# Cross-attention on one core: a third plain fp32 value unit in the first batch, its head's loads exchanged between two queues, first and last batch in a new order

## The chip, the core and the metric

One core of a Trainium2 chip runs the whole kernel: TensorE (PE: matrix products; PEld is its weight load), VectorE (DVE), ScalarE (ACT), GpSimd (POOL), and SyncE (SP), which issues most loads and stores. The metric is the device time of one execution in microseconds (us). Lower is better.

## The reference

Eight batches. For each one, with x1 and x2 of 512 channels x 1024 positions, all fp32:

```python
q = einsum('bcn,dc->bnd', x1, Wq) + bq          # 64 channels
k = einsum('bcn,dc->bdn', x2, Wk) + bk[:, None]
v = einsum('bcn,dc->bdn', x2, Wv) + bv[:, None] # 512 channels
attn = softmax(einsum('bnd,bdm->bnm', q, k), axis=2)
return einsum('bcm,bnm->bcn', v, attn) + x1
```

## The kernel before, in words

Every step is a short method of `Batch`, named by a letter or two, and the program is three strings of such words, FIRST (line 30, batch 0), MIDDLE (line 49, batches 1 to 6) and LAST (line 66, batch 7). `follow` (line 533) calls them in that order. Each engine runs its own instructions strictly in the order of the words; engines wait for each other through semaphores. `+` before a word means the next batch and `-` the one before, so the strings overlap the batches by hand.

A batch has eight units of 128 positions. Numbers behind a dot are a unit (0 to 7), a quarter of 256 positions (0 to 3), a pair of units (0 to 3) or a half of 512 (0, 1).

- **Loads.** `hx` (163) loads x2's first quarter in four pieces of 128 KB, `hw` (168) Wv in four of 256 KB; `lwq` (173) loads the q and k weights (and bqk, their bias), `ldx2` (156) and `ldx1` (144) the rest of x2 and x1, `lsd` (177) bv. In `begin` (515) `hx` goes on SP's queue and `hw` on ScalarE's, then ten warm-up products on TensorE follow. A DMA may wait before it is issued, since the semaphores of DMAs are used in turn and each must be free again.
- **q and k.** `Q` and `K` (221, 240) project them, as plain fp32 products of 64 columns. `qe`/`ke` evict them from PSUM on ScalarE, `qd`/`kc` copy them to the other half of the partitions by DMA, `qr`/`kr` and `ql`/`kl` split each number into a high part (ScalarE) and a low part (VectorE).
- **Values.** A unit of v is 128 positions x 512 channels over four blocks of 128 input channels. Usually x2 is split by `xh` (ScalarE), `xl`, `xd` (VectorE), one quarter at a time, the weights by `wh`, `wl`, `wd`, `w4`, and a unit takes three passes of fp32r products: `VX` (394) two of them, 8 products, into a bank X, `VY` (391) one, 4 products, into a bank Y that ScalarE first fills with the bias (`sy`, 380) and copies out afterwards (`cy`, 399). `jn` (403) joins X and Y on VectorE. In batch 0, units 0 and 1 instead are plain fp32 products of the raw data (`VF`, 363), 4 products a unit without any split, joined by `jf` (377).
- **v split.** `vh` (ScalarE), `vl`, `vd` (VectorE) split v, pair by pair, for the output.
- **Scores and softmax.** `S.h.i` (259) makes scores of 128 keys x 512 positions from two products, `Sc` copies them to SBUF (ScalarE), `F` takes the maximum over the blocks of keys (VectorE), `T` over the partitions (GpSimd), `L` subtracts (VectorE), `E` takes the exponential (ScalarE), `H`, `l`, `d` split it. `es`, `a1`, `a2`, `a3`, `tot`, `few`, `rec`, `r2` make the sums and their reciprocals.
- **Output.** `R.u.m` (431) does three fp32r products for unit u and key block m; in batch 0 units 0 and 1 use plain fp32 (`RF`, 448). `oy`, `o`, `oa`, `st` scale, add x1 (a DMA that accumulates, from GpSimd) and store. In the last batch `lt` (479) loads x1 for the last two units instead.

Buffers come from pools whose counts stand in `BUFS` (line 119); three PSUM banks X, three Y and two "sc" are shared by all products.

Of the kernel before, what the change touches and what calls it, by code (L numbers as in the profile page):

```python
# [36 lines left out]
S.1.7 a1.0 Sc.1.6 RF.0.1 RF.0.2 RF.0.3 RF.0.4 Sc.1.7 F.2 RF.0.5 +ldx2.0 +qd +qr +ql sy.7 VY.7 cy.7 jn.7 vh.3  # L37
T.2 L.4 E.2 H.2 a2.0 a3.0 +ldx2.1 +K +ke +kc RF.1.0 L.5 vl.3 vd.3 tot.0 few.0 RF.1.1 RF.1.2 RF.0.6 RF.0.7 l.2
d.2 E.3 H.3 es.1 l.3 a1.1 d.3 E.5 RF.1.3 RF.1.4 E.4 H.4 es.2 rec.0 r2.0 of.0 oa.0 st.0 RF.1.5 RF.1.6 RF.1.7
R.2.0 R.2.1 R.2.2 H.5 R.2.3 F.3 R.2.4 R.2.5 R.2.6 R.2.7 R.3.0 R.3.1 a2.1 a3.1 +kr +kl +S.0.0 +S.0.1 +Sc.0.0  # L40
+Sc.0.1 R.3.2 of.1 R.3.3 l.4 T.3 L.7 E.7 H.7 d.4 +S.0.2 +Sc.0.2 R.3.4 R.3.5 R.3.6 l.5 l.7 +S.0.3 +Sc.0.3 a1.2
a2.2 a3.2 L.6 +S.0.4 +Sc.0.4 R.3.7 +S.0.5 +Sc.0.5 R.4.0 R.4.1 +S.0.6 tot.1 few.1 rec.1 d.5 d.7 oa.1 st.1 tot.2
few.2 +S.0.7 R.4.2 R.4.3 R.4.4 R.4.5 R.4.6 R.4.7 r2.1 oy.2 oy.3 o.2 o.3 oa.2 oa.3 st.3 +Sc.0.6 +Sc.0.7 +F.0
E.6 H.6 es.3 l.6 a1.3 d.6 rec.2 r2.2 oy.4 st.2 +T.0 +L.0 +L.1 +E.0 +E.1 +es.0 +F.1 o.4 oa.4 st.4 a2.3 a3.3
R.5.0 R.5.1 R.5.2 R.5.3 R.5.4 R.5.5 R.5.6 R.5.7 oy.5 o.5 oa.5 st.5 +xh.0 +xl.0 +xh.2 +xl.2 +xd.0 +xh.1 +xl.1
# [26 lines left out]
vl.3 a3.1 vd.3 R.0.6 R.1.6 R.0.7 R.1.7 H.3 r2.0 T.2 L.4 L.5 E.4 E.5 es.2 d.2 R.2.0 R.2.1 R.2.2 R.2.3 R.2.4
R.2.5 R.2.6 R.2.7 F.3 l.3 oy.0 o.0 tot.1 few.1 rec.1 lt a1.2 H.5 d.3 R.3.0 R.3.1 R.3.2 R.3.3 R.3.4 R.3.5 R.3.6
R.3.7 oy.1 o.1 T.3 L.7 E.7 oa.0 st.0 oa.1 L.6 l.5 d.5 R.5.0 R.5.1 R.5.2 R.5.3 R.5.4 R.5.5 R.5.6 R.5.7 E.6 es.3
a1.3 st.1 a2.2 a3.2 tot.2 few.2 r2.1 oy.2 o.2 oa.2 st.2 H.4 l.4 d.4 R.4.0 R.4.1 R.4.2 R.4.3 R.4.4 R.4.5 R.4.6
R.4.7 oy.3 o.3 oa.3 a2.3 a3.3 tot.3 few.3 H.6 l.6 st.3 d.6 R.6.0 R.6.1 R.6.2 R.6.3 R.6.4 R.6.5 R.6.6 R.6.7
# [6 lines left out]
def kernel(  # L83
# [47 lines left out]

    class Batch:
# [214 lines left out]
        def chunk(self, k):  # L347
            return self.x2[k // 2][:, k % 2]

        def xh(self, k):  # L350
            self.c[k] = {"h": new([P, CT, QN], "kh", f"xh_{self.b}_{k}", FR)}
            nc.scalar.activation(self.c[k]["h"], self.chunk(k), AF.Copy, scale=-SPLIT)

        def xl(self, k):
            self.c[k]["l"] = new([P, CT, QN], "kl", f"xl_{self.b}_{k}", FR)
            nc.vector.tensor_tensor(self.c[k]["l"], self.chunk(k), f32(self.c[k]["h"]), ALU.add)

        def xd(self, k):
# [2 lines left out]
            nc.vector.scalar_tensor_tensor(c["d"], f32(c["l"]), T, f32(c["h"]), ALU.mult, ALU.add)
# [153 lines left out]
    def begin():  # L515
        for c in range(CT):
            states[0].hx(c)
            states[0].hw(c)
# [1 line left out]
        nc.vector.memset(spark, 0.0)  # L520

        for i, times in enumerate((4, 3, 3)):
            ps = bank("Y", f"ps_warm{i}")
            for k in range(times):
                nc.tensor.matmul(
                    ps, warm, warm.unsqueeze(1).to_broadcast([P, 4, P]), start=(k == 0), stop=(k == times - 1)
                )
# [48 lines left out]
```

## Time and profile before

| | us |
|---|---|
| median of three runs (660.91, 660.78, 661.68) | 660.91 |
| the profiled execution's own time | 661.69 |
| its span, first to last instruction | 659.9 |
| TensorE busy | 652.8 (99%) |
| VectorE busy | 619.0 (94%) |
| ScalarE busy | 452.4 (69%) |
| GpSimd busy | 203.5 (31%) |

A row of the timeline has the start, the time, the engine with its line, the operation, what it writes and reads, the shape, and in brackets the idle time before it and what ended it; rows of equal neighbours are merged (x4). The chain that ended last is followed back from the last instruction, at each step to what released it. A plain fp32 product shows as two TensorE passes, an fp32r product as one. Passes overlap: a pass takes longer than the distance to the next.

### The profile page before, as it was taken

What the parts mean: (1) busy time and instruction counts of PE and PEld (TensorE: products, weight loads), DVE (VectorE), ACT (ScalarE), POOL (GpSimd) and SP (SyncE); (2) the same over time, 40 slices, a digit from 0 to 9 for tenths busy, and PEclk for the clock granted to TensorE, in tenths of its full rate; (3) what the DMA queues carried; (4) which work ended last, traced back from release to release, by engine and by line L of the source; (5) the groups of instructions that cost most, each with busy time, mean ns of one, the idle gap of its engine ahead of it and who ended that gap; (6) DMA issues with size and microseconds to landing.
All of it is one profiled execution on the core that took longest, in us unless ns stands there. A gap on an engine that the chain in (4) does not pass through costs nothing.

```text
span 659.9 us, 8059 instructions
## 1 busy us (share of the span) xinstructions
PE 652.8 (99%) x2802; PEld 492.4 (75%) x2802; DVE 619.0 (94%) x689; ACT 452.4 (69%) x670; POOL 203.5 (31%) x162
## 2 busy tenths in 40 slices
...
GB/s 316 191 96 107 119 98 221 73 201 96 129 175 112 175 98 163 124 173 120 114 173 96 216 100 111 173 83 224 81 128 179 77 207 98 126 81 49 93 150 124
DMA packets 41464, 90.21 MB, mean 137 GB/s; under 512 B 13136, under 2 KB 13904, under 8 KB 37712
## 3 DMA queue, kind: packets, MB, share of 16 engines
...
q8 instruction: 22, 0.36, 0.2%
q14 instruction: 18, 0.15, 0.1%
HBM read 51.91 MB, written 16.78 MB: 104 GB/s over the span
## 4 chain that ended last, share of the span: by engine, by line
PE 96%; DMA 2%; ACT 1%; DVEq 0%; issue 0%; ACTq 0%; DVE 0%
PE ps_oX L426 34%; PE ps_oY L426 17%; PE ps_vX L386 17%; PE ps_s L262 9%; PE ps_vY L386 8%; PE ps_k L205 4%; PE ps_q L205 4%; PE ps_o L451 2%; DMA x<-in_x_dram 1%; DMA w_raw<-in_wvT_dram 1%; ACT eh L297 0%; ACT e L293 0%; ACT ps_vY L382 0%; ACT vy L401 0%; ACT es L312 0%; ACT vh L408 0%
## 5 line engine op out<-in xcount | busy, mean ns | idle before, releaser
L426 PE MATMUL ps_oY<-vd,ed 128*128 128x512 f32 x496 | 193.2, 392 | 0.0
L426 PE MATMUL ps_oX<-vh,eh 128*128 128x512 f32 x496 | 193.0, 389 | 0.0
L426 PE MATMUL ps_oX<-vl,el 128*128 128x512 f32 x496 | 193.0, 389 | 0.0
L426 PEld LDWEIGHTS ps_oY<-vd,ed 128*128 128x128 f32 x496 | 93.1, 188 | 25.0 <-issue 5.1
L506 POOL DMA_DIRECT2D o<-in_x1T_dram x62 | 55.6, 916 | 171.6 <-ACT o L503 97.6
L426 PEld LDWEIGHTS ps_oX<-vl,el 128*128 128x128 f32 x496 | 93.1, 188 | 19.5
L426 PEld LDWEIGHTS ps_oX<-vh,eh 128*128 128x128 f32 x496 | 93.1, 188 | 19.3 <-issue 0.2
L293 ACT ACTIVATE e<-e 128x1024 f32<-128x1024 f32 x64 | 67.9, 1062 | 49.6 <-DVE e L290 48.3
L267 ACT COPY e<-ps_s 128x512 f32<-128x512 f32 x128 | 70.9, 589 | 28.6 <-PE ps_s L262 27.6
L329 POOL PARTITION_ALL_REDUCE den<-es x32 | 80.7, 2522 | 26.0 <-DVE es L319 25.0
L306 DVE SCALAR_TENSOR_TENSOR ed<-el,eh 128x1024 fp32r<-128x1024 f32 x62 | 83.0, 1341 | 2.1
...
L301 DVE TENSOR_TENSOR el<-e,eh 128x1024 fp32r<-128x1024 f32 x62 | 79.5, 1298 | 0.0
L290 DVE TENSOR_TENSOR e<-e,top 128x1024 f32<-128x1024 f32 x64 | 77.0, 1231 | 0.0
...
L386 PE MATMUL ps_vX<-wh,xh 128*128 128x512 f32 x248 | 67.6, 394 | 0.0
L386 PE MATMUL ps_vY<-wd,xd 128*128 128x512 f32 x248 | 65.9, 393 | 0.8 <-ACT ps_vY L382 0.8
L386 PE MATMUL ps_vX<-wl,xl 128*128 128x512 f32 x248 | 66.3, 389 | 0.0
L297 ACT ACTIVATE eh<-e 128x1024 fp32r<-128x1024 f32 x62 | 64.6, 1054 | 0.5
L401 ACT COPY vy<-ps_vY 128x512 f32<-128x512 f32 x62 | 36.4, 591 | 40.0 <-PE ps_vY L386 38.8
L386 PEld LDWEIGHTS ps_vX<-wh,xh 128*128 128x128 f32 x248 | 45.8, 188 | 15.7 <-DVE max L277 4.1
L386 PEld LDWEIGHTS ps_vY<-wd,xd 128*128 128x128 f32 x248 | 46.2, 188 | 12.5 <-ACT ps_vY L382 1.6
...
## 6 DMA issues: line engine op xcount, KB each, us to landing
...
```

Source lines behind the costliest of these rows:

```text
L205: nc.tensor.matmul(ps[r, :], wqk_sb[:, which, c, :], x(h, c), start=(c == 0), stop=(c == CT - 1))
L262: nc.tensor.matmul(ps, k[:, ts(i, P)], self.qa[:, ts(h, H)], start=(z == 0), stop=(z == 1))
L267: nc.scalar.copy(self.half[h][:, :, i, :], self.ps[h, i].rearrange("p (q n) -> p q n", q=2))
L290: nc.vector.tensor_tensor(e, e, top, ALU.subtract)
L293: nc.scalar.activation(self.unit(u), self.unit(u), AF.Exp)
L297: nc.scalar.activation(self.e[u]["h"], self.unit(u), AF.Copy, scale=SPLIT)
L301: nc.vector.tensor_tensor(self.e[u]["l"], self.unit(u), f32(self.e[u]["h"]), ALU.subtract)
L306: nc.vector.scalar_tensor_tensor(e["d"], f32(e["l"]), -T, f32(e["h"]), ALU.mult, ALU.add)
L329: nc.gpsimd.partition_all_reduce(self.den[Q], self.es[Q][:, 0, :], P, ReduceOp.add)
L386: nc.tensor.matmul(ps, self.c[j // 2][z][:, c, ts(j % 2, P)], w[z][:, c, :], start=(start and c == 0), stop=(stop and c == CT - 1), skip_g ...
L426: nc.tensor.matmul(ps, self.e[u][z][:, m, :], self.v[m // 2][z][:, m % 2, :], start=start, stop=stop, skip_group_check=True,)
L506: nc.gpsimd.dma_start(self.o[u], x1T[self.b, ts(u, P), :], accum_op=ALU.add)
```

## The change

Four things are changed together.

1. **VF.2.** In batch 0 unit 2 becomes a plain fp32 unit too: VF.2.0 to VF.2.3 and jf.2 come, VX.2, VY.2, sy.2, cy.2 and jn.2 go. x2's second quarter (units 2 and 3) is then split for unit 3 alone: `apart` (a new method) gives its second 128 positions in batch 0, and xh.1, xl.1, xd.1 work on that half.
2. **Queues.** `hx` is issued by ScalarE, `hw` by SP; bqk is loaded by ScalarE behind the four `hx`.
3. **FIRST** in a new order. Among much else: all twelve VF words stand ahead of K, and nothing between K and Q on TensorE; x2's second quarter is loaded ahead of the q and k weights; after Q TensorE has VY.3, VX.3, VX.5, VX.4, VY.4, VY.5; vl.0 and vd.0 come after vd.1 and jn.4; jn.5 comes behind the first quarter's maximum, VX.6 ahead of the second's.
4. **LAST** in a new order: H.0 early, H.1 late, S.1.2 and S.1.4 between VY.3 and VY.4, lt earlier.

MIDDLE is as it was.

```diff
 FIRST = """
-VF.0.0 VF.1.0 VF.1.1 wh.0 VF.1.2 VF.1.3 wl.0 wd.0 w4.0 wh.1 wl.1 wd.1 w4.1 VF.0.1 VF.0.2 VF.0.3 lwq ldx2.0
-ldx2.1 xh.1 lsd K xl.1 xh.2 xh.3 ldx1.0 bv ke xd.1 xl.2 xl.3 VX.2 ldx1.1 jf.0 xd.2 xd.3 sy.2 sy.3 sy.5 jf.1 Q
-kc VY.2 VY.3 qe kr cy.2 cy.3 vh.0 qd kl jn.2 vl.0 qr sy.4 VX.3 jn.3 vh.1 VX.4 VY.5 cy.5 vd.0 VX.5 VY.4 cy.4 ql
-S.0.0 S.0.1 S.0.2 S.0.3 S.0.5 Sc.0.0 Sc.0.1 Sc.0.2 Sc.0.3 S.0.4 Sc.0.4 Sc.0.5 S.0.6 Sc.0.6 S.0.7 Sc.0.7 S.1.1
-sy.6 vl.1 vd.1 +ldx1.0 jn.4 jn.5 vh.2 S.1.0 Sc.1.0 Sc.1.1 VX.7 +ldx1.1 +Q +qe S.1.2 Sc.1.2 VY.6 cy.6 F.0 vl.2
-vd.2 S.1.5 S.1.3 Sc.1.3 T.0 L.0 E.0 F.1 S.1.6 S.1.4 Sc.1.4 Sc.1.5 L.1 E.1 es.0 VX.6 jn.6 RF.0.0 T.1 L.2 L.3
+VF.0.0 VF.0.1 VF.1.0 wh.0 wl.0 wd.0 w4.0 VF.1.1 wh.1 VF.0.2 wl.1 VF.0.3 w4.1 ldx2.0 xh.1 xl.1 xd.1 VF.1.2
+VF.1.3 wd.1 VF.2.0 VF.2.1 VF.2.2 VF.2.3 lwq ldx2.1 lsd K xh.2 xh.3 ldx1.0 bv ke xl.2 xl.3 ldx1.1 jf.0 jf.2
+xd.3 sy.3 sy.4 sy.5 jf.1 Q kc VY.3 qe kr cy.3 vh.0 qd kl VX.3 jn.3 vh.1 qr +ldx1.0 VX.5 VX.4 xd.2 VY.4 VY.5
+cy.4 cy.5 vl.1 ql S.0.0 S.0.1 S.0.2 S.0.3 Sc.0.0 Sc.0.1 vd.1 S.0.4 Sc.0.2 Sc.0.3 Sc.0.4 jn.4 S.0.5 Sc.0.5
+S.0.6 Sc.0.6 vl.0 vd.0 S.0.7 Sc.0.7 F.0 T.0 S.1.1 VX.6 sy.6 VY.6 cy.6 jn.6 jn.5 vh.2 S.1.0 Sc.1.0 Sc.1.1 L.0
+E.0 +ldx1.1 +Q +qe S.1.2 Sc.1.2 S.1.3 Sc.1.3 VX.7 S.1.4 Sc.1.4 RF.0.0 RF.0.1 S.1.6 F.1 S.1.7 S.1.5 RF.0.2
...
 LAST = """
-VY.0 VX.0 cy.0 jn.0 VX.1 VY.1 T.1 L.2 cy.1 jn.1 VX.2 VX.3 VX.4 sy.2 VY.2 S.1.2 L.3 a1.0 a2.0 H.1 l.1 xd.3 E.2
-vh.0 vl.0 d.1 E.3 es.1 sy.3 VY.3 H.0 l.0 cy.2 jn.2 sy.4 VY.4 cy.3 jn.3 d.0 a3.0 Sc.1.2 a1.1 vd.0 sy.5 vh.1
-vl.1 a2.1 S.1.4 vd.1 S.1.3 Sc.1.3 Sc.1.4 tot.0 few.0 cy.4 jn.4 -r2.3 -os.6 -oa.6 -st.6 VY.5 cy.5 VX.5 jn.5
+VY.0 VX.0 cy.0 jn.0 VX.1 VY.1 T.1 L.2 cy.1 jn.1 VX.2 VX.3 VX.4 sy.2 VY.2 xd.3 L.3 H.0 E.2 sy.3 VY.3 vh.0 l.0
+S.1.2 E.3 es.1 vl.0 a1.0 H.2 d.0 cy.2 vd.0 S.1.4 a2.0 sy.4 VY.4 cy.3 jn.2 jn.3 l.2 Sc.1.2 a3.0 sy.5 S.1.3 sy.6
+vh.1 vl.1 lt a1.1 a2.1 cy.4 jn.4 Sc.1.3 Sc.1.4 vd.1 -r2.3 -os.6 -oa.6 -st.6 VY.5 cy.5 VX.5 jn.5 VX.6 S.1.5 H.1
...
         def hx(self, c):
...
-            nc.sync.dma_start(self.x2[0][:, 0, c, :], x2[0, :, 0, c])
+            nc.scalar.dma_start(self.x2[0][:, 0, c, :], x2[0, :, 0, c])
...
         def hw(self, c):
...
-            nc.scalar.dma_start(wraw[c // 2][:, c % 2, :], wvT[c])
+            nc.sync.dma_start(wraw[c // 2][:, c % 2, :], wvT[c])
 
         def lwq(self):
             nc.sync.dma_start(wqk_sb, wqk)
-            nc.sync.dma_start(bqk_sb, bqk)
...
+        def apart(self, k):
+
+            return slice(P, QN) if self.first and k == 1 else slice(0, QN)
+
         def xh(self, k):
+            at = self.apart(k)
             self.c[k] = {"h": new([P, CT, QN], "kh", f"xh_{self.b}_{k}", FR)}
-            nc.scalar.activation(self.c[k]["h"], self.chunk(k), AF.Copy, scale=-SPLIT)
+            nc.scalar.activation(self.c[k]["h"][:, :, at], self.chunk(k)[:, :, at], AF.Copy, scale=-SPLIT)
...
         for c in range(CT):
             states[0].hx(c)
             states[0].hw(c)
+        nc.scalar.dma_start(bqk_sb, bqk)
```

`xl` and `xd` take the same slice `at` as `xh`.

More of the change, by code (lines that the diff above doesn't have):

```diff
@@ L36 @@
-vd.2 S.1.5 S.1.3 Sc.1.3 T.0 L.0 E.0 F.1 S.1.6 S.1.4 Sc.1.4 Sc.1.5 L.1 E.1 es.0 VX.6 jn.6 RF.0.0 T.1 L.2 L.3
[L37 to L45, printed above, removed]
@@ L46 @@
-+xd.1 R.6.0 R.6.1 R.6.2 R.6.3 R.6.4 R.6.5 R.6.6 R.6.7 oy.6 o.6 +sy.0 R.7.0 R.7.1 R.7.2 R.7.3 R.7.4 R.7.5 R.7.6
-R.7.7 oy.7 o.7 +xh.3 +S.1.1 +xd.2 +xl.3 +S.1.0 +Sc.1.0 +Sc.1.1 tot.3 few.3 rec.3 +sy.1
+VF.0.0 VF.0.1 VF.1.0 wh.0 wl.0 wd.0 w4.0 VF.1.1 wh.1 VF.0.2 wl.1 VF.0.3 w4.1 ldx2.0 xh.1 xl.1 xd.1 VF.1.2
+VF.1.3 wd.1 VF.2.0 VF.2.1 VF.2.2 VF.2.3 lwq ldx2.1 lsd K xh.2 xh.3 ldx1.0 bv ke xl.2 xl.3 ldx1.1 jf.0 jf.2
+xd.3 sy.3 sy.4 sy.5 jf.1 Q kc VY.3 qe kr cy.3 vh.0 qd kl VX.3 jn.3 vh.1 qr +ldx1.0 VX.5 VX.4 xd.2 VY.4 VY.5
@@ new lines @@
+cy.4 cy.5 vl.1 ql S.0.0 S.0.1 S.0.2 S.0.3 Sc.0.0 Sc.0.1 vd.1 S.0.4 Sc.0.2 Sc.0.3 Sc.0.4 jn.4 S.0.5 Sc.0.5
+S.0.6 Sc.0.6 vl.0 vd.0 S.0.7 Sc.0.7 F.0 T.0 S.1.1 VX.6 sy.6 VY.6 cy.6 jn.6 jn.5 vh.2 S.1.0 Sc.1.0 Sc.1.1 L.0
+E.0 +ldx1.1 +Q +qe S.1.2 Sc.1.2 S.1.3 Sc.1.3 VX.7 S.1.4 Sc.1.4 RF.0.0 RF.0.1 S.1.6 F.1 S.1.7 S.1.5 RF.0.2
+RF.0.3 RF.0.4 L.1 E.1 es.0 RF.0.5 +ldx2.1 Sc.1.5 Sc.1.6 Sc.1.7 vl.2 vd.2 T.1 L.2 L.3 E.3 F.2 RF.1.0 H.3 l.3
+d.3 RF.1.1 RF.1.2 +ldx2.0 +K a1.0 a2.0 a3.0 E.2 H.2 es.1 l.2 a1.1 sy.7 VY.7 +qd +qr +ql RF.1.3 RF.1.4 RF.1.5
@@ new lines @@
+d.2 cy.7 jn.7 RF.0.6 RF.1.6 RF.0.7 RF.1.7 +ke +kc R.2.0 vh.3 T.2 L.4 L.5 E.4 E.5 H.4 H.5 F.3 tot.0 few.0 rec.0
+r2.0 of.0 of.1 oa.0 oa.1 st.0 l.4 R.2.1 R.2.2 R.2.3 R.2.4 R.2.5 R.3.0 R.3.1 es.2 a1.2 a2.1 a3.1 R.3.2 R.3.3
+d.4 vl.3 R.3.4 +kr +kl +S.0.0 +S.0.1 +Sc.0.0 +Sc.0.1 R.3.5 +S.0.2 +Sc.0.2 +S.0.3 +Sc.0.3 vd.3 R.2.6 R.3.6
+R.2.7 R.3.7 +S.0.5 T.3 L.6 L.7 E.6 E.7 H.6 l.5 d.5 R.4.0 R.4.1 a2.2 tot.1 few.1 rec.1 r2.1 a3.2 tot.2 few.2
+es.3 a1.3 l.6 st.1 oy.2 o.2 oa.2 st.2 H.7 d.6 +S.0.4 +Sc.0.4 +Sc.0.5 l.7 oy.3 o.3 oa.3 st.3 R.4.2 R.4.3 R.4.4
@@ L48 @@
+R.4.5 R.4.6 R.4.7 +S.0.7 d.7 +S.0.6 +Sc.0.6 +Sc.0.7 +F.0 +xh.0 +xl.0 +xd.0 a2.3 rec.2 r2.2 oy.4 +T.0 +L.0 +L.1
+o.4 oa.4 st.4 R.5.0 R.5.1 R.5.2 R.5.3 R.5.4 R.5.5 R.5.6 R.5.7 oy.5 o.5 oa.5 st.5 a3.3 +E.1 +F.1 +xh.2 +xl.2
+R.6.0 R.6.1 R.6.2 R.6.3 R.6.4 R.6.5 R.6.6 R.6.7 oy.6 o.6 R.7.0 R.7.1 R.7.2 R.7.3 +sy.0 +xh.1 +xl.1 +xd.1 +E.0
++es.0 +sy.1 +S.1.0 +S.1.1 +xd.2 +xh.3 +Sc.1.0 +xl.3 +Sc.1.1 tot.3 few.3 rec.3 R.7.4 R.7.5 R.7.6 R.7.7 oy.7 o.7
 """
@@ L66 @@
 LAST = """
-VY.0 VX.0 cy.0 jn.0 VX.1 VY.1 T.1 L.2 cy.1 jn.1 VX.2 VX.3 VX.4 sy.2 VY.2 S.1.2 L.3 a1.0 a2.0 H.1 l.1 xd.3 E.2
-vh.0 vl.0 d.1 E.3 es.1 sy.3 VY.3 H.0 l.0 cy.2 jn.2 sy.4 VY.4 cy.3 jn.3 d.0 a3.0 Sc.1.2 a1.1 vd.0 sy.5 vh.1
-vl.1 a2.1 S.1.4 vd.1 S.1.3 Sc.1.3 Sc.1.4 tot.0 few.0 cy.4 jn.4 -r2.3 -os.6 -oa.6 -st.6 VY.5 cy.5 VX.5 jn.5
-VX.6 H.2 l.2 S.1.5 Sc.1.5 sy.7 sy.6 S.1.7 rec.0 vh.2 vl.2 S.1.6 Sc.1.6 Sc.1.7 F.2 -os.7 -oa.7 -st.7 VX.7 VY.6
-cy.6 jn.6 VY.7 cy.7 jn.7 R.0.0 R.0.1 R.0.2 R.0.3 R.1.0 R.1.1 R.1.2 R.1.3 vd.2 R.0.4 R.1.4 R.0.5 R.1.5 vh.3
@@ L72 @@
[L72 to L76, printed above, removed]
@@ L77 @@
-rec.2 H.7 l.7 r2.2 oy.4 oy.5 o.4 o.5 oa.4 oa.5 st.4 st.5 d.7 R.7.0 R.7.7 rec.3 r2.3 oy.6 oy.7 t.6 t.7 o.6 o.7
-st.6 st.7 p.7 sq.7
+VY.0 VX.0 cy.0 jn.0 VX.1 VY.1 T.1 L.2 cy.1 jn.1 VX.2 VX.3 VX.4 sy.2 VY.2 xd.3 L.3 H.0 E.2 sy.3 VY.3 vh.0 l.0
+S.1.2 E.3 es.1 vl.0 a1.0 H.2 d.0 cy.2 vd.0 S.1.4 a2.0 sy.4 VY.4 cy.3 jn.2 jn.3 l.2 Sc.1.2 a3.0 sy.5 S.1.3 sy.6
+vh.1 vl.1 lt a1.1 a2.1 cy.4 jn.4 Sc.1.3 Sc.1.4 vd.1 -r2.3 -os.6 -oa.6 -st.6 VY.5 cy.5 VX.5 jn.5 VX.6 S.1.5 H.1
+l.1 S.1.6 Sc.1.5 Sc.1.6 a3.1 d.1 vh.2 vl.2 tot.0 few.0 sy.7 S.1.7 Sc.1.7 F.2 -os.7 -oa.7 -st.7 VX.7 VY.6 cy.6
```

19 lines of the change are left out of this document (15 added, 4 removed).

## The prediction

> **What bounds the kernel now.** I read the page first: span, then the busy shares.
>
> ```profile
> span 659.9 us, 8059 instructions
> PE 652.8 (99%) x2802; PEld 492.4 (75%) x2802; DVE 619.0 (94%) x689; ACT 452.4 (69%) x670; POOL 203.5 (31%) x162
> ```
>
> TensorE is busy all but 7 us, so any time to be had lies in its few waits or in the work it is given. The view of waits, for TensorE alone, names them:
>
> ```profile
> PE ps_k L205 <- DMA x<-in_x_dram: 1.4, 1, 1.4
> PE ps_warm L525 <- DVE spark L520: 1.0, 1, 1.0
> PE ps_vY L386 <- ACT ps_vY L382: 0.8, 1, 0.8
> PE ps_s L262 <- ACT e L267: 0.2, 1, 0.2
> ```
>
> One wait is for a load, in the head, before the K projection; the other two stand in the last batch. The table of stretches says where another engine is as full as TensorE (columns: stretch and length, then busy time of PE, PEld, DVE, ACT, POOL, clock, DMA share, GB/s).
>
> ```profile
> 4.84:12.00 7.16, 7.16 (x17) 2.77 (x15) 3.73 (x4) 4.49 (x6) 0.00 (x0) 1.00 1.00 355
> ...
> 33.00:60.00 27.00, 27.00 (x105) 15.42 (x104) 24.18 (x30) 20.85 (x33) 7.55 (x5) 1.00 0.39 110
> 60.00:105.00 45.00, 45.00 (x185) 34.36 (x184) 44.34 (x48) 32.32 (x47) 20.52 (x17) 1.00 0.57 112
> 105.00:589.00 484.00, 484.00 (x2125) 374.05 (x2124) 471.30 (x524) 341.06 (x508) 153.81 (x120) 1.00 0.57 138
> 589.00:627.00 38.00, 36.99 (x159) 29.19 (x158) 36.53 (x42) 27.76 (x42) 11.13 (x8) 1.00 0.30 62
> ```
>
> The six middle batches (105 to 589) have no TensorE gap at all, and the change does not touch their order: what is won ahead of them is carried through, as long as VectorE keeps up. It is nearly full from 60 on (44.34 of 45.00).
>
> The chain that ended last, from the start to the first scores, is the path that the change edits (start, length, piece):
>
> ```profile
> 1.17 4.39 DMA w_raw<-in_wvT_dram
> 5.57 8.90 DMA x<-in_x_dram
> ...
> 14.51 3.65 PE ps_k L205 x14
> 18.16 2.04 PE ps_vX L386 x8
> 20.20 3.58 PE ps_q L205 x16
> 23.78 2.04 PE ps_vY L386 x8
> 25.82 3.63 PE ps_vX L386 x16
> 29.44 0.91 PE ps_vY L386 x4
> 30.35 1.81 PE ps_vX L386 x8
> 32.16 0.91 PE ps_vY L386 x4
> 33.07 2.95 PE ps_s L262 x13
> ```
>
> Two plain fp32 value units end at 12.00; then K waits for the load of x2's second half (issued at 5.57, landed at 14.47), runs to 18.16, and from there TensorE has no wait up to the scores at 33.07. Fourteen of K's sixteen passes stand behind that wait; Q, next to it, shows what sixteen take in one go (3.58).
>
> **The change, part by part.**
>
> *Third fp32 unit.* VX.2 goes (2.04, the row at 18.16) and so does VY.2, half of the row at 23.78, 1.02. VF.2 comes in front of K: four products, each shown as two TensorE passes. The nearest row in number is that of the fp32 output passes, from the same chain read to 100 us:
>
> ```profile
> 58.35 8.78 PE ps_o L451 x20
> ```
>
> 0.439 us a pass, so eight passes are 3.5. (The sixteen passes of the two present units, with short waits, take 7.16, or 3.6 a unit.) VF.2 therefore costs TensorE 0.4 to 0.5 more than the two pieces that it replaces.
>
> The Trainium skill, "FP8 and Floating Point Precision", section TensorE Precision Notes, says that true FP32 takes four passes through the array, which speaks against the edit: a split unit takes three. With one split pass at 1.81/8 = 0.227 us, four passes for each of four products would be 3.63, an estimate by that page, and the sum below 0.13 worse; the rows (two passes of 0.439 a product) are close to it, and I keep them.
>
> *What VF.2 covers.* It needs x2's second quarter and stands where K now waits. From 12.00 to 18.16 are 6.16; K without a wait takes what Q takes, 3.58. So 2.58 of wait and of a broken first step go, if x2's second half is there when VF.2 ends, at 12.00 + 3.5 = 15.5. It landed at 14.47: 1.0 to spare. New times: K 15.5 to 19.1, Q 19.1 to 22.7 (now 23.78).
>
> Sum on TensorE up to the scores: -2.04 - 1.02 - 2.58 + 3.5 = **-2.14**.
>
> *Does the score side follow?* The scores also need q to be evicted, copied across, rounded and split. The rows now (ScalarE, then VectorE):
>
> ```profile
> 23.83 1.40 ACT L212 ACTIVATE q<-ps_q,bqk_sb 64x512 f32<-64x512 f32 x2 [2.59 <-PE ps_q L205]
> 25.25 1.06 ACT L251 ACTIVATE kh<-k 128x1024 fp32r<-128x1024 f32 x1
> ...
> 29.78 1.06 ACT L235 ACTIVATE qa<-q 128x1024 fp32r<-128x1024 f32 x1 [1.41 <-DMA q<-q]
> ```
>
> ```profile
> 15.24 1.22 DVE L361 SCALAR_TENSOR_TENSOR xd<-xl,xh 128x1024 fp32r<-128x1024 f32 x1
> ...
> 26.34 1.23 DVE L255 TENSOR_TENSOR kl<-k,kh 128x1024 fp32r<-128x1024 f32 x1 [4.13 <-ACT kh L251]
> ...
> 31.39 1.22 DVE L238 TENSOR_TENSOR qa<-q,qa 64x1024 fp32r<-64x1024 f32 x1
> 32.64 1.23 DVE L413 SCALAR_TENSOR_TENSOR vl<-vh,v 128x1024 fp32r<-128x1024 f32 x1
> 33.90 1.23 DVE L418 TENSOR_TENSOR vd<-vh,vl 128x1024 fp32r<-128x1024 f32 x1
> 35.05 1.28 DVE L404 SCALAR_TENSOR_TENSOR v<-ps_vX,vy 128x512 f32<-128x512 f32 x2
> 36.25 0.68 DVE L275 TENSOR_TENSOR max<-e 128x512 f32<-128x512 f32 x1
> ...
> 48.32 0.69 DVE L404 SCALAR_TENSOR_TENSOR v<-ps_vX,vy 128x512 f32<-128x512 f32 x1 [1.42 <-PE ps_vX L386]
> ```
>
> In the new order: q evicted 22.7 to 24.15 (1.45 after Q's end, as now), kh to 25.2, kl to 26.45, jn.3 (0.64 each, row 35.05) to 27.1, vh.1 (about 1.06 like kh) to 28.2, qa to 29.2; on VectorE xd.2 27.1 to 28.3, vl.1 to 29.5, then ql to 30.75. TensorE has VY.3, VX.3, VX.5, VX.4, VY.4, VY.5 in between: 1.02 + 3.63 + 1.81 + 2 x 0.91 = 8.3, and is ready at 31.0. So q's side just fits. Now qa started 4.55 after the eviction's end, held by q's copy. If it does so again, qa starts at 28.7 instead of 28.2, ql ends at 31.25 at the worst, and the scores wait 0.2. I take +0.1 (0 to 0.25).
>
> *Loads exchanged.* x2's first quarter goes to ScalarE's queue and Wv to SP's. The bytes stay. wqk, now issued fifth, comes behind the last Wv piece (which waits for the first load's landing) and x2's second quarter; bqk's small load leaves SP. From the DMA view up to 30 us (40 slices of 0.75 us):
>
> ```profile
> DMA  0026999999897999999999942019400000799989
> GB/s 0 0 42 190 300 356 382 391 395 354 284 360 257 333 410 391 404 431 399 429 421 421 421 197 87 33 49 208 98 0 0 0 0 0 167 199 191 279 355 448
> ```
>
> The engines are full from 3.0 to 17.25 and idle by 18.75, so a hole that wqk leaves moves later loads by at most its 256 KB at about 390 GB/s, 0.65. K has 1.0 of room for that. Q, which now starts at 20.20 with all loads in, would start at 19.1: the row lets it wait from 0 to (20.20 - 19.1) = 1.1, plus the shift. As the traffic has ended by 18.75, I take +0.1. The first unit's start at 4.84 depends on one load of each queue before and after: 0, give or take 0.3.
>
> *Half split, sy.2, cy.2.* Half of xl.1 and xd.1 leave VectorE (2 x 0.6), half of xh.1 and two PSUM copies leave ScalarE; both idle in the head (VectorE 4.13 before kl). Nothing by itself.
>
> *Order of the first batch.* VectorE must be earlier too, since it has no room from 60 on. vl.0 and vd.0 (1.26 + 1.15 from start to start) now stand between ql and the first maximum: ql's end 30.75 + vd 1.15 + jn 0.64 + 1.26 + 1.15 = 34.95, against 36.25, a lead of 1.3. jn.5 (0.64) is put behind it, and the 1.42 that it lost at 48.32 for VX.6 goes, VX.6 being moved ahead of the second quarter's maximum: 1.3 - 0.6 + 1.4 = 2.1, as much as TensorE's lead. I take +0.15 given back (0 to 0.7, if the idle time isn't won).
>
> *Last batch.* Its longest wait is for a seed copy (sy.4) on ScalarE; its second for a score copy:
>
> ```profile
> 599.24 0.50 ACT ps_vY L382
> ...
> 606.91 0.60 ACT e L267
> ```
>
> In the new order ScalarE has the same nine pieces between cy.1 and sy.4 (sy.2, two H, two E, vh.0, es.1, sy.3, cy.2), so sy.4 comes no sooner; TensorE has one more score pair (S.1.4, 2 x 0.227 = 0.45) to fill the wait. The later waits, and the VectorE that is full here (36.53 of 38.00), can take that back. 0, between -0.45 and +0.45. lt, earlier on SP, lands long before its use; the tail is the same.
>
> **Sum:** -2.14 + 0.1 + 0.1 + 0.15 = -1.8 against the profiled execution's own 661.69 (its span 659.9 and 1.8 around it): 659.9. The median of the three runs is 660.91, 0.8 lower, and one of the three was 661.68. If the runs at 660.8 had a shorter wait for the load, the new order, which has room there, comes out at 659.9 all the same; if the 0.8 lies elsewhere, at 659.1. Against the median that is -1.0, 0.15%, and 0.2% (1.3 us) is about what a measurement of this kernel can tell from no change.
>
> **Rivals.**
>
> *Loads decide* (no gain beyond what the queue gives). For it: Q needs x1's tiles 1.1 earlier than any row shows them needed, and wqk goes later. Against it: the DMA engines are idle by 18.75. Price: 0.5 to 1.1 at Q, so 660.4 to 661.0.
>
> *The last batch gains too.* For it: TensorE lost 38.00 - 36.99 = 1.0 there, of which S.1.4 alone fills 0.45, and H.0 ahead of H.1 lets the first split units come earlier. Against it: VectorE is nearly full there. Price: 0.45 to 1.0 more, 658.9 to 659.4.
>
> *Slower: VectorE falls behind in batch one.* vl.0 and vd.0 were ahead of ql and are now between ql and the first maximum (2.4), while only jn.5 (0.64) leaves. If the scores start no earlier than now (Q held until 21.3, over 2 us by late loads), the first maximum comes 0.6 later than now (ql's end to it: 3.64 now, 32.61 to 36.25; 4.2 then), jn.5 adds 0.6 behind it, and VectorE, with 0.66 of room from 60 to 105, hands it to TensorE. It decides from a lead of the scores under 0.6. Price: 0.6 to 1.2 over the profiled time, 662.3 to 662.9. Against it: TensorE's own sum up to the scores is certain but for the loads.
>
> **How the numbers follow.** Forecast 0.60, for 659.0 to 660.6 around 659.9; of this 0.24 lies under 659.6, more than 0.2% below the median, and 0.36 above. Loads decide 0.12 (within 0.2%). Last batch gains too 0.17 (faster). VectorE behind 0.11 (slower). Faster 0.41, same 0.48, slower 0.11. The range 658.8 to 661.2 leaves out the slower rival and the ends of the others.
>
> **What would show it.** Right: K follows VF.2 without a wait, near 15.5; Q ends near 22.7; the first scores near 31.0 with less than 0.3 of wait; second batch's first units 1.8 earlier than now, and the same lead at the last batch. Wrong: a wait of K or Q for x (loads), a gap of TensorE between 60 and 105 put down to VectorE's kl, el or ed (rival three), less than 0.6 or more than 1.5 of TensorE's idle time from 589 to 627 (rival two, or its opposite).

## The result and the profile after

The changed kernel takes **662.51 us** (median of 22 runs, 661.65 to 662.98), the kernel before, measured beside it, 660.91 (22 runs, 659.43 to 662.22): a ratio of 1.0023, 95% interval [1.0016, 1.0029], so 0.23% or 1.6 us slower. 659.9 was forecast.

The page of the changed kernel, its span and busy shares:

```profile
span 660.6 us, 8048 instructions
PE 653.9 (99%) x2798; PEld 491.8 (74%) x2798; DVE 617.3 (93%) x689; ACT 450.8 (68%) x668; POOL 199.1 (30%) x162
```

Its profiled execution took 662.40, so it stands at the median; that of the kernel before (661.69) stands 0.8 above its own.

The head came out as forecast. The chain of the changed kernel up to the scores (start, length, piece):

```profile
5.43 10.37 PE ps_v L373 x24
15.80 3.58 PE ps_k L204 x16
19.38 3.43 PE ps_q L204 x16
22.81 1.13 PE ps_vY L393 x4
23.94 5.44 PE ps_vX L393 x24
29.39 1.82 PE ps_vY L393 x8
31.21 4.13 PE ps_s L261 x18
```

No wait for a load is left; K, Q and the scores start at 15.80, 19.38 and 31.21 (forecast 15.5, 19.1 and 31.0). K's 0.3 comes from the first unit: by the timeline it starts at 5.22, 0.38 after the 4.84 of before, where the prediction allowed 0.3 either way. But new waits stand later. TensorE's waits in the changed kernel, behind that of the warm-up (total, times, longest):

```profile
PE ps_s L261 <- DVE kl L254: 0.7, 1, 0.7
PE ps_vY L393 <- ACT ps_vY L389: 0.7, 2, 0.4
PE ps_s L261 <- ACT e L266: 0.5, 2, 0.3
PE ps_oY L433 <- DVE ed L305: 0.2, 1, 0.2
```

To see where the lead went, take the same product in both traces. TensorE's rows of the kernel before (start, length, line, product):

```profile
66.56 0.79 PE L426 MATMUL ps_oY<-vd,ed 128*128 128x512 f32 x1
...
118.53 0.39 PE L262 MATMUL ps_s<-qa,kh 128*128 128x512 f32 x1
...
118.99 1.14 PE L386 MATMUL ps_vY<-wd,xd 128*128 128x512 f32 x4
...
160.17 0.39 PE L262 MATMUL ps_s<-qa,kl 128*128 128x512 f32 x1
...
526.41 1.08 PE L205 MATMUL ps_q<-x,wqk_sb 128*64 128x512 f32 x4
...
655.82 0.39 PE L426 MATMUL ps_oX<-vl,el 128*128 128x512 f32 x1
```

The same six in the changed kernel, with the idle time just before them:

```profile
64.76 0.79 PE L433 MATMUL ps_oY<-vd,ed 128*128 128x512 f32 x1
...
117.26 0.50 PE L261 MATMUL ps_s<-qa,kh 128*128 128x512 f32 x1 [0.32 <-ACT e L266]
...
118.24 0.96 PE L393 MATMUL ps_vY<-wd,xd 128*128 128x512 f32 x3 [0.24 <-ACT ps_vY L389]
...
160.37 0.50 PE L261 MATMUL ps_s<-qa,kl 128*128 128x512 f32 x1 [0.68 <-DVE kl L254]
...
527.25 1.08 PE L204 MATMUL ps_q<-x,wqk_sb 128*64 128x512 f32 x4
...
656.52 0.39 PE L433 MATMUL ps_oX<-vl,el 128*128 128x512 f32 x1
```

Subtracted, the changed kernel's TensorE is 1.80 ahead at 65, 1.27 at 118.5 and 0.75 at 119; at 160 it is 0.20 behind and 0.31 one product later (160.71 against 160.40), at 526 0.84, at the last product 0.70. The losses are 1.05 in batch 1 near 118, 1.06 up to and at 160, and then 0.53 with **no wait at all**, 0.1 a batch. The last batch gives 0.14 back. Three losses, and so three causes to look for.

### The profile page after: what moved, and what is told of

Same layout as the page of the kernel before. It is cut to its first block, busy times and chain, and to the rows that moved or that the text cites. A ratio compares the mean times of both kernels' runs of the same rounds, so it can differ in the third digit from the quotient of the medians.

```text
span 660.6 us, 8048 instructions
## 1 busy us (share of the span) xinstructions
PE 653.9 (99%) x2798; PEld 491.8 (74%) x2798; DVE 617.3 (93%) x689; ACT 450.8 (68%) x668; POOL 199.1 (30%) x162
## 4 chain that ended last, share of the span: by engine, by line
PE 77%; DVE 13%; ACT 4%; DMA 3%; issue 2%; POOL 0%; SPq 0%; DVEq 0%; POOLq 0%; ACTq 0%
PE ps_oX L433 27%; PE ps_oY L433 14%; PE ps_vX L393 13%; PE ps_s L261 7%; PE ps_vY L393 7%; PE ps_k L204 3%; PE ps_q L204 3%; DVE e L289 3%; DVE el L300 2%; PE ps_v L373 2%; DVE vd L425 1%; DVE ed L305 1%; DVE vl L420 1%; DVE max L276 1%; DMA out_dram<-o 1%
## 5 line engine op out<-in xcount | busy, mean ns | idle before, releaser
L328 POOL PARTITION_ALL_REDUCE den<-es x32 | 79.3, 2477 | 21.2 <-DVE es L318 18.2
L305 DVE SCALAR_TENSOR_TENSOR ed<-el,eh 128x1024 fp32r<-128x1024 f32 x62 | 80.2, 1294 | 2.0
L393 PE MATMUL ps_vX<-wh,xh 128*128 128x512 f32 x244 | 66.2, 393 | 0.0
L281 POOL PARTITION_ALL_REDUCE top<-max x32 | 45.4, 1417 | 66.7 <-DVE max L277 66.7
L393 PE MATMUL ps_vY<-wd,xd 128*128 128x512 f32 x244 | 64.3, 391 | 0.7 <-ACT ps_vY L389 0.7
```

The source lines that it names most:

```text
L281: nc.gpsimd.partition_all_reduce(self.top[Q], self.fold[Q][:, 0, :], P, ReduceOp.max)
L305: nc.vector.scalar_tensor_tensor(e["d"], f32(e["l"]), -T, f32(e["h"]), ALU.mult, ALU.add)
L328: nc.gpsimd.partition_all_reduce(self.den[Q], self.es[Q][:, 0, :], P, ReduceOp.add)
L393: nc.tensor.matmul(ps, self.c[j // 2][z][:, c, ts(j % 2, P)], w[z][:, c, :], start=(start and c == 0), stop=(stop and c == CT - 1), skip_g ...
```

## The experiments

| kernel | median | before, beside it | ratio, 95% interval |
|---|---|---|---|
| 1 third unit alone | 661.37 | 660.86 | 1.0007 [0.9999, 1.0016] |
| 2 changed, VectorE relieved | 662.48 | 660.86 | 1.0021 [1.0013, 1.0030] |
| 3 before, VectorE relieved | 661.06 | 660.86 | 1.0001 [0.9990, 1.0012] |
| 4 changed, xd.2 early | 662.52 | 660.86 | 1.0024 [1.0015, 1.0033] |
| 5 changed, two more ScalarE instructions | 661.73 | 661.02 | 1.0005 [0.9996, 1.0014] |
| 6 before, the same two | 662.11 | 661.02 | 1.0012 [1.0003, 1.0021] |
| 7 changed, vd.3 lower | 661.62 | 661.02 | 1.0008 [1.0000, 1.0017] |
| 8 changed, one store later | 661.74 | 661.02 | 1.0007 [0.9998, 1.0016] |
| 9 changed, edits 5, 7 and 8 | 660.22 | 661.45 | 0.9976 [0.9967, 0.9985] |
| 10 third unit and exchanged queues | 660.37 | 661.45 | 0.9979 [0.9967, 0.9991] |
| 11 exchanged queues alone | 662.72 | 661.45 | 1.0019 [1.0006, 1.0031] |
| 12 changed, old last batch | 662.58 | 661.45 | 1.0018 [1.0007, 1.0030] |
| 13 exchanged queues, two more instructions | 661.52 | 660.75 | 1.0012 [1.0003, 1.0022] |
| 14 old order with the new head and last batch | 659.81 | 660.75 | 0.9982 [0.9973, 0.9991] |

The kernel before came out between 660.75 and 661.45 beside them, so the ratios are what to compare; the changed kernel's is 1.0023.

### The first theory: VectorE sets the pace (1 to 4)

VectorE is 43.87 of 45.00 full from 60 to 105 and is only 0.7 ahead at 109, where TensorE is 1.8 ahead. Its row there, the join jn.0 of batch 1, in the kernel before and in the changed one:

```profile
109.87 0.67 DVE L404 SCALAR_TENSOR_TENSOR v<-ps_vX,vy 128x512 f32<-128x512 f32 x1
...
109.16 0.68 DVE L411 SCALAR_TENSOR_TENSOR v<-ps_vX,vy 128x512 f32<-128x512 f32 x1
```

The rivals were ScalarE's order, and that no lead is ever kept.

**1. The third unit in the old order** (the words that differ).

```diff
-VF.0.3 lwq ldx2.0 ldx2.1 xh.1 lsd K
+VF.0.3 ldx2.0 lwq ldx2.1 xh.1 lsd VF.2.0 VF.2.1 VF.2.2 VF.2.3 K
-VX.2
-sy.2
-VY.2
-cy.2
-jn.2
+jf.2
```

> The kernel before with the third plain fp32 unit alone (x2's second quarter loaded ahead of wqk so that the unit needs not wait; the split of that quarter stays whole, the queues and the rest of the order stay). Theory 1, VectorE sets the pace from the scores to the second batch: the K eviction, kh and kl come 1.0 earlier, jn.2 (0.6) leaves VectorE behind kl and nothing is put there, so VectorE leads by about 1.6 and TensorE by 2.1, and most of it is kept: 659.3 to 660.2, and VectorE's lead at the start of the second batch is 1.3 to 1.7 where the full change has 0.7. Theory 2, the order of ScalarE's copies makes the waits of the second batch: the old order keeps them away, same time, but VectorE's lead does not matter. Theory 3, a lead won in the head is never carried to the end: 660.9 as before.

The ratio is 1.0007. The time alone is that of the third theory, which the trace refutes. The longest of TensorE's waits is a new one:

```profile
PE ps_v L366 <- DMA w_raw<-in_wvT_dram: 1.4, 1, 1.4
```

With the old queues the units wait for Wv, which eats most of the gain; 0.24 of lead over the profile of before is left at the scores. That 0.24 is the same, within 0.1, at every later product up to the end. So the order of before does carry a lead, only a smaller one than the first two theories had.

**2 and 3. VectorE relieved in the first batch**, in the changed kernel and in that before. One of four steps of the maximum is left out in batch 0:

```diff
-            for g in (4, 6):
+            for g in (4,) if self.first else (4, 6):
```

> The changed kernel with the last of the four folding steps of the score maximum left out in the first batch alone (the maximum is taken over six of the eight blocks there): four VectorE instructions of 0.72 less, 2.9 in all, no other engine's work changed. Theory 1 (VectorE sets the pace): its lead at 109 is no longer 0.7 but as large as TensorE's 1.8, the waits at 117 to 119 (1.0) go, that for kl at 160 (0.86) goes or comes smaller: 660.6 to 661.5. Theory 2 (ScalarE's order): the waits at 117 to 119 stay, 662.5. Theory 3 (a lead is never carried): the waits go and others come, 662.0 to 662.5.

> The kernel before with the same step left out in its first batch (maximum over six of eight blocks). There TensorE has no wait from 31 to 598, so 2.9 of VectorE time less can bring nothing there: 660.6 to 661.2 by every theory. A gain over 0.4 would say that VectorE already holds the kernel before in a way that its view of waits does not show.

**4. One VectorE instruction moved into idle time** (the words that differ).

```diff
-xd.3 sy.3 sy.4
+xd.3 xd.2 sy.3 sy.4
-VX.4 xd.2 VY.4
+VX.4 VY.4
```

> The changed kernel with one VectorE instruction, xd.2 (1.14 from start to start), moved from behind kl into VectorE's idle 5.05 ahead of kl, right behind xd.3, where the kernel before has it. Theory 1 (VectorE sets the pace): VectorE leads by 1.8 at 109 and TensorE keeps its 1.8 through 119: 661.0 to 661.7. Theory 2 and 3: 662.3 to 662.6.

2 and 4 changed nothing (1.0021 and 1.0024), nor did 3 (1.0001), where every theory had it so. TensorE's waits from 105 to 185 in the relieved kernel (2), then its VectorE:

```profile
PE ps_s L261 <- DVE kl L254: 0.7, 1, 0.7
PE ps_s L261 <- ACT e L266: 0.3, 1, 0.3
PE ps_vY L393 <- ACT ps_vY L389: 0.2, 1, 0.2
```

```profile
39.13 1.29 DVE L411 SCALAR_TENSOR_TENSOR v<-ps_vX,vy 128x512 f32<-128x512 f32 x2 [1.75 <-ACT vy L408]
...
52.69 1.23 DVE L300 TENSOR_TENSOR el<-e,eh 128x1024 fp32r<-128x1024 f32 x1 [1.27 <-ACT eh L296]
...
82.77 0.75 DVE L498 SCALAR_TENSOR_TENSOR o<-ps_oX,r,oy 128x512 f32<-128x512 f32 x1 [0.51 <-ACT oy L484]
```

The same three waits, to a tenth. VectorE spends what it was given waiting for ScalarE at 39 and 52, and waits for it at 82 as the changed kernel does. **The first theory is refuted as far as these runs reach**: room for VectorE ahead of 82 wins nothing. They do not test the stretch from 82 to 109, and TensorE does come down there to VectorE's lead (see 8). Something else had to be late at the same three places.

### Three side effects, one experiment each (5 to 9)

**The loss at 160.** The timeline of the changed kernel there, then of the kernel before (idle time ahead of an instruction in brackets):

```profile
155.92 1.05 ACT L311 COPY es<-e 128x1024 f32<-128x1024 f32 x1 [0.36 <-ACT e L292]
156.87 1.06 ACT L250 ACTIVATE kh<-k 128x1024 fp32r<-128x1024 f32 x1
...
157.96 2.36 DVE L254 TENSOR_TENSOR kl<-k,kh 128x1024 fp32r<-128x1024 f32 x1
157.96 1.99 POOL L328 PARTITION_ALL_REDUCE den<-es  x1
```

```profile
156.33 1.05 ACT L312 COPY es<-e 128x1024 f32<-128x1024 f32 x1
...
158.46 1.22 DVE L255 TENSOR_TENSOR kl<-k,kh 128x1024 fp32r<-128x1024 f32 x1
158.65 2.69 POOL L329 PARTITION_ALL_REDUCE den<-es  x1
159.60 2.12 DVE L306 SCALAR_TENSOR_TENSOR ed<-el,eh 128x1024 fp32r<-128x1024 f32 x1
```

In the changed kernel the copy es.3 starts 0.36 after the instruction ahead of it (0.07 in the kernel before), kh comes late with it, and kl then starts together with GpSimd's sum and takes 2.36. In the kernel before kl is ahead of the sum by 0.19 and takes 1.22; the lengthened one is ed, for which TensorE does not wait. So 0.3 of ScalarE decides which instruction meets the sum. Where are the 0.3 from? Number all of ScalarE's rows in the trace (waits included, from 0): es.3's wait is row 190 in the changed kernel and row 188 in that before; there the same gap of 0.3 stands at row 318, 128 rows on, ahead of es.0 of batch 3.

**5 and 6. The place in ScalarE's stream**, moved by two in both kernels:

```diff
         nc.scalar.activation(spark, spark, AF.Exp)
+        nc.scalar.mul(spark, spark, 1.0)
+        nc.scalar.mul(spark, spark, 1.0)
```

> The changed kernel with two tiny ScalarE instructions (a multiplication of the 128x1 spark tile by 1) added at the very start, where ScalarE idles. In the changed kernel the third seed-sum copy of batch two (es.3, at 155.92) starts 0.32 after its wait has ended, in the kernel before 0.04; kh and kl come later by that, and kl then runs while GpSimd's sum does (2.36 instead of 1.22); TensorE waits 0.7 for it. That copy stands on a multiple of 64 of ScalarE's instructions, in the kernel before the same 0.32 is found 128 instructions later. Theory A (the place in the instruction stream makes the 0.3): two more instructions move it away, es.3 starts without the 0.3, kl takes 1.22, the wait at 160 goes: 661.6 to 661.8 instead of 662.5. Theory B (it comes from what es.3 waits for, in this order of work): no change, 662.3 to 662.6.

> The kernel before with the same two tiny ScalarE instructions at its start. They put es.3 of batch two on the place where it stands in the changed kernel. Theory A: es.3 waits the 0.3, kl runs into GpSimd's sum (over 2 us), TensorE waits 0.5 to 0.9 for it near 160 and the end comes that much later: 661.4 to 661.8 instead of 660.9. Theory B: 660.6 to 661.1.

Both went with theory A, though 6 by its ratio alone: its median lies over that theory's range. The timeline of the changed kernel with the two more, where kl is ahead of the sum again:

```profile
155.29 1.05 ACT L311 COPY es<-e 128x1024 f32<-128x1024 f32 x1
...
157.42 1.22 DVE L254 TENSOR_TENSOR kl<-k,kh 128x1024 fp32r<-128x1024 f32 x1
```

and of the kernel before with them, where the gap appears and TensorE waits:

```profile
155.16 1.05 ACT L312 COPY es<-e 128x1024 f32<-128x1024 f32 x1 [0.36 <-ACT e L293]
...
157.20 2.36 DVE L255 TENSOR_TENSOR kl<-k,kh 128x1024 fp32r<-128x1024 f32 x1
...
159.62 0.50 PE L262 MATMUL ps_s<-qa,kl 128*128 128x512 f32 x1 [0.73 <-DVE kl L255]
```

Two instructions that compute nothing needed take 0.8 (by the medians) to 1.2 (by the ratios) from one kernel and add 0.8 (by the ratio) to 1.1 (by the medians) to the other. In the sixteen profiles of this study es.3 of batch 1 has the gap in the eight in which its wait is row 190, and in no other.

**7. The loss without waits.** From 160 on the passes lengthen, not the gaps: of TensorE's 64 passes a batch that read vd, 16 (as many as read the fourth pair's tile, vd.3) are followed by the next pass after 0.234 instead of 0.227. In the changed kernel vd.3's first use makes it the last buffer to be placed; it lies at byte 224832 of each partition, in the kernel before at 217536. The group of all passes that read vd, from 215 to 580 (busy us, mean ns), first in the changed kernel, then with the buffer reserved earlier; in the kernel before it is 121.2 as well:

```profile
L433 PE MATMUL ps_oY<-vd,ed 128*128 128x512 f32 x310 | 121.6, 392 | 0.0
```

```profile
L435 PE MATMUL ps_oY<-vd,ed 128*128 128x512 f32 x310 | 121.2, 391 | 0.0
```

```diff
             nc.vector.tensor_tensor(v["d"], f32(v["h"]), f32(v["l"]), ALU.subtract)
+            if self.first and p == 2:
+                new([P, 2, C], "vd3", "vd_hold", FR)
```

> The changed kernel with the buffer of the fourth pair's difference tile (vd.3) reserved earlier, so that it lies at 217536 in each partition as in the kernel before, and three output tiles at the top instead of it; the order of work is the same. In the changed kernel it lies at 224832, at the top, and the 16 passes of each batch that read it take 0.234 instead of 0.227. Theory C (the place makes the 7 ns): those passes take 0.227, no drift of 0.1 a batch: 16 x 7.2 ns x 7 = 0.8 less, 661.6 to 661.9. Theory D (the 7 ns belong to the order of work or to the run): unchanged, 662.3 to 662.6.

Theory C: a ratio 0.0015 lower, and TensorE's distance to the kernel before stays the same from 160 to 600 (0.2 to 0.3 ahead at both ends of the middle batches) where in the changed kernel it grew 0.1 a batch.

**8. The loss at 118.** The chain there runs back from the seed copy (sy, which fills a bank Y with the bias) through ScalarE's vh.0, which idles 0.92 for VectorE's jn.1, along VectorE to o.7 and rec.3, and from there to SP's queue. The timeline of the changed kernel:

```profile
100.25 2.47 SPq L517 DMA_DIRECT2D out_dram<-o  x2
...
102.81 1.92 SPq L333 DMA_DIRECT2D few<-den  x2
...
108.36 0.17 DVE L337 RECIPROCAL r<-few 128x2 f32<-128x2 f32 x1 [0.52 <-DMA few<-den]
108.56 0.69 DVE L498 SCALAR_TENSOR_TENSOR o<-ps_oX,oy 128x512 f32<-128x512 f32 x1
...
112.75 1.06 ACT L415 ACTIVATE vh<-v 128x1024 fp32r<-128x1024 f32 x1 [0.92 <-DVE v L411]
```

The sum that few.3 copies is ready at 99.9 (GpSimd, 97.56 with 2.34); the copies are issued at 102.81, behind a store that waits for its transfer, and take 4.9 and 5.3 to land. The store is moved behind them (the words that differ):

```diff
-oa.5 st.5 a3.3
+oa.5 a3.3
-tot.3 few.3 rec.3
+tot.3 few.3 st.5 rec.3
```

> The changed kernel with one issue on SP's queue moved: the store st.5 of batch one goes behind the small copies few.3, which stand behind it now and with it wait for the transfer into o.5 (to 102.37), though their sum is ready at 99.9. VectorE's rec.3 waits 0.5 for few.3 at 108.36, o.7 and ScalarE's cy.0 come behind it, and from there the chain runs to the seed copy for which TensorE waits at 118. Theory E (that queue holds the second batch's start): rec.3 finds few.3 landed, the waits at 117 to 119 (1.0) shrink by about 0.5: 661.9 to 662.2. Theory F (VectorE, without a gap from 82 to 108, or ScalarE would be there no sooner): the 0.5 goes elsewhere, 662.4 to 662.6.

Theory E, and more than half of it: the copies go at 101.27 and land after 3.1 and 3.5, rec.3 does not wait, and both waits near 118 are gone. The only wait of TensorE that the view still lists from 105 to 185 is that for kl, 0.6.

It is not the whole loss. With 8 TensorE leads the kernel before by 1.49 at 109 and by 1.17 at 119 (changed kernel 1.81 and 0.75), and VectorE's jn.0 leads by 1.13 (0.71). In 9 the pair is 0.89 and 0.85: from 119 on TensorE has in each of these profiles, to 0.05, the lead that VectorE has at 109. As the view lists no wait of VectorE from 84 to 109 in 8 and 9, the 0.3 to 0.4 that is still lost there is its own lateness, as the first theory had it. That part is read from the traces; no run changes VectorE's work in that stretch.

**9. The three edits together.**

> The changed kernel with the three edits together: two tiny ScalarE instructions at the start, vd.3 at its old place, st.5 behind few.3. Alone they gave 661.73, 661.62 and 661.74 against the changed kernel's 662.5. Theory A+C+E (three separate losses): they add, about 2.1 by the traces' pieces (0.86 at 160, 0.72 of drift, 0.5 at 118), 2.4 by the medians: 660.0 to 660.4, and TensorE's lead of the head is kept to the last batch but for some 0.5 at 118. Rival (VectorE, full from 60 to 210, takes back what one of them gives): 660.9 to 661.5.

They add: 0.9976 of the kernel before, 0.0047 below the changed kernel's ratio (alone 0.0018, 0.0015 and 0.0016). TensorE no longer waits for kl; of 1.26 of lead at 107 (in this profile Q took 4.05 and not 3.43) 0.8 to 0.9 reach the last batch, the rest going at 118 to a seed copy, down to VectorE's lead as told under 8.

```profile
PE ps_vY L393 <- ACT ps_vY L389: 0.6, 2, 0.4
...
```

### The parts of the change (10 to 14)

**10 and 11. The queues**, with the third unit in the old order and alone: `hx` on ScalarE's queue, `hw` on SP's, bqk's load on ScalarE's, as in the change; 10 has the words of 1 as well.

```diff
-            nc.sync.dma_start(self.x2[0][:, 0, c, :], x2[0, :, 0, c])
+            nc.scalar.dma_start(self.x2[0][:, 0, c, :], x2[0, :, 0, c])
-            nc.scalar.dma_start(wraw[c // 2][:, c % 2, :], wvT[c])
+            nc.sync.dma_start(wraw[c // 2][:, c % 2, :], wvT[c])
-            nc.sync.dma_start(bqk_sb, bqk)
+        nc.scalar.dma_start(bqk_sb, bqk)
```

> The kernel before with the third plain fp32 unit and the exchanged queues, in the old order. With the old queues the units waited 1.4 for Wv, the scores 0.2 for q, and what was left was kept to the end (661.37 in the median, where the kernel before has 660.9). Here vd.3, es.3 and few.3 stand as in the kernel before. Theory (the head's gain is real, and the new order of the first batch loses it by three side effects): the wait for Wv goes, 660.0 to 660.4. Rival 1 (the exchange of the queues doesn't serve the third unit, or the old order makes the scores wait for q instead): 660.7 to 661.3. Rival 2 (no lead lasts beyond the second batch): 660.9 with a wait between 105 and 180.

> The kernel before with the loads of the head exchanged between the two queues and nothing else. If the exchange costs nothing by itself: 660.7 to 661.1, K held by x's second half until 13.2 to 14.5 as before. If the old queues' load wait of K is what makes the kernel before come out at 660.5 in some runs and 661.7 in others, the exchange changes that share: all near one of the two.

10 is faster than both kernels; the rest of its lead, 0.74 at the scores, is the same to 0.1 at the last product. 11 is slower, which neither expectation had, though no load is later than in the profile of before. Against that profile it is level up to 159 (to 0.05) and 1.06 behind from 163 on. Two of TensorE's waits in 11:

```profile
PE ps_k L204 <- DMA x<-in_x_dram: 1.3, 1, 1.3
...
PE ps_s L261 <- DVE kl L254: 0.7, 1, 0.7
```

kl takes 2.36 here too: bqk's issue and one more wait, ahead of wh.0, have put es.3's wait on row 190.

**13. 11 with the two more instructions of 5.**

> The kernel before with the exchanged queues alone (which came out 0.19% slower, with es.3 starting 0.3 late and kl at 2.36, though no load was later) and the two tiny ScalarE instructions at the start. If the exchange costs only by the place of es.3 in ScalarE's stream, which one more issue on that queue has shifted: es.3 starts without the 0.3, no wait for kl, a ratio of 0.998 to 1.000 to the kernel before. If the exchange itself costs (loads, queues): still 1.0015 to 1.0025.

The ratio lies between the two expectations. The wait for kl is gone; what stays (1.0012) goes with K's wait for x, 0.9 in its profile. In other runs of the old queues that wait is shorter: the profile of experiment 6 has none (K from 13.09 to 16.69, before to 18.16). The intervals of 11 and 13 overlap, so how the 0.19% divide is not settled.

**12. The old last batch in the changed kernel** (the whole string LAST; here its first words alone):

```diff
-VY.0 VX.0 cy.0 jn.0 VX.1 VY.1 T.1 L.2 cy.1 jn.1 VX.2 VX.3 VX.4 sy.2 VY.2 xd.3 L.3 H.0
+VY.0 VX.0 cy.0 jn.0 VX.1 VY.1 T.1 L.2 cy.1 jn.1 VX.2 VX.3 VX.4 sy.2 VY.2 S.1.2 L.3 a1.0
```

> The changed kernel with the old order of the last batch. By the two traces the new order takes 0.2 less from 553 to the last product (the changed kernel is 0.88 behind there and 0.70 at the end): 662.6 to 662.8. If the new last batch were a part of the loss: 661.5 to 662.2.

1.0018 against 1.0023, within the intervals: the last batch moves nothing that can be told.

**14. The old order with the third unit, exchanged queues, the new first words up to K and the new last batch** (the words up to K, against the kernel before; x2's second quarter is split whole).

```diff
-VF.0.0 VF.1.0 VF.1.1 wh.0 VF.1.2 VF.1.3 wl.0 wd.0 w4.0 wh.1 wl.1 wd.1 w4.1 VF.0.1 VF.0.2 VF.0.3
+VF.0.0 VF.0.1 VF.1.0 wh.0 wl.0 wd.0 w4.0 VF.1.1 wh.1 VF.0.2 wl.1 VF.0.3 w4.1 ldx2.0 xh.1 xl.1 xd.1
+VF.1.2 VF.1.3 wd.1 VF.2.0 VF.2.1 VF.2.2 VF.2.3 lwq ldx2.1 lsd
...
```

> The old order of the first batch with the third fp32 unit and the exchanged queues, and with the new order's first words (up to K) and its last batch. With the old first words the three units took 11.06 from 5.43 on, with the new ones 10.37 in the changed kernel; the new last batch takes 0.2 less in the trace. No side effect of the three is there (es.3, vd.3 and few.3 stand as in the kernel before). If the pieces add: 0.8 less than with the old first words and last batch, a ratio of 0.996 to 0.9975. If the scores then wait for q (0.2 there already) or VectorE takes it back: 0.9975 to 0.9985.

The fastest median, 659.81. Its stretches (60 to 105, and the middle batches):

```profile
60.00:105.00 45.00, 45.00 (x188) 35.01 (x187) 44.33 (x49) 31.69 (x46) 19.27 (x16) 1.00 0.59 118
105.00:585.00 480.00, 480.00 (x2108) 370.79 (x2107) 467.29 (x518) 339.01 (x504) 153.90 (x120) 1.00 0.58 139
```

No gap in TensorE. The scores start at 31.11, 1.8 ahead of the kernel before, and its last product at 653.90, 1.9 ahead. That is 1.2 more than 10 has at the end, so by the traces the pieces add, as the first expectation had it. By the ratios they do not: 14 is 0.18% faster than the kernel before, and 9 and 10 are as good within the intervals. The runs do not settle which holds.

## Why the prediction was wrong, by its own steps

- **Third unit, -2.14: right.** The three units took 10.37 in the profile, 3.46 a unit (3.5 forecast). By the four passes that the prediction cited from the Trainium skill, "FP8 and Floating Point Precision", section TensorE Precision Notes, an estimate of 3.63 was given; the trace is nearer to the row. K followed without a wait, Q ended at 22.81 (22.7), the scores came near 31.0.
- **The base of the sum: right, and it mattered.** The sum was made on an execution in which K waited 1.4 for x and which stands 0.8 above its median. Of the two readings that the prediction left open the profiles fit the first: the wait varies (1.4, 0.6 in the profile of 3, none in that of 6), so of the 1.8 won against that profile about 1.0 is won against the median.
- **"What is won ahead of them is carried through": right as a rule, wrong here.** Experiments 1, 10 and 14 carry 0.24, 0.74 and 1.7 to the end. In the changed kernel the lead of 1.8 at 109 is 0.84 of delay at 526, and so the last of the signs that the prediction named for being right stayed away. Its condition, that VectorE keeps up, failed at one place: at 109 VectorE leads by 0.71, and TensorE comes down from 1.8 to that. The other two losses are not VectorE's pace.
- **Order of the first batch, +0.15 (0 to 0.7): the step that failed first.** It was worked out on VectorE's ops alone, and only to 48. The loss is 1.05 at 118. About 0.7 of it starts at a store on SP's queue ahead of two copies of 512 bytes (8); the 0.3 to 0.4 that is left, VectorE's own, lies within the stated range. The prediction costed the move of steps on VectorE but not what they were moved past on SP.
- **Loads exchanged, +0.1: right for the loads, wrong for what moves with them.** "bqk's small load leaves SP" was costed at nothing where it arrives. There it is an instruction; together with the copies that left and the waits that came, ScalarE's stream shifted by two rows, and that cost about 1 (5, 6, 11). No row of before could price it, though its gap of 0.3 at row 318 stood in the trace.
- **Nothing for the tiles' places.** A new order of first uses moved vd.3: 0.1 a batch, 0.7 in all by the traces, 1.0 by the ratio (7). No step spoke of it.
- **Last batch, 0: right** (0.14 in the traces, 12).
- **The rival "slower: VectorE falls behind in batch one"**, 662.3 to 662.9, has the time but not the path: the scores led by 1.8, far over its limit of 0.6, and TensorE has no gap between 60 and 105, where its sign was. That 662.5 falls into its range is luck.

By the traces, -1.80 + 1.05 + 1.06 + 0.53 - 0.14 = +0.70; with the 0.8 of the base and 0.1 of the changed kernel's own execution it is the 1.6 of the medians. Without the three side effects the changed kernel (9) comes to 659.3 by its ratio and 660.2 by its median, with the forecast's 659.9 between them. The half split of x2's second quarter and the rest of the new order were not run by themselves.
